# Gated attention: the output of block 2 by seven products, the ranking cut into pieces between its additions

## The chip, the cores and the metric

The kernel runs on one core of a Trainium2 chip. The metric is the device time of one execution in microseconds (us), the median of several runs. The engines are TensorE (PE, with its weight loads as PEld), VectorE (DVE), ScalarE (ACT), GpSimd (POOL) and the queue that issues most transfers (SP). Each engine works through its own list of instructions in order, and waits where an instruction needs something of another engine.

## The reference, cut to what matters

Two layers, each of attention and a feed-forward part with a layer norm behind each, on an input of 2 × 1024 rows of 512. The change lies in the second layer, between its gated attention and its feed-forward part:

```python
go = o @ Wog.T + x @ Wig.T
on = o * lax.rsqrt(jnp.mean(o * o, axis=-1, keepdims=True) + EPS) * g_norm_w
o = on * (go * jax.nn.sigmoid(go))
return o @ Wo.T                       # the gated attention's output, added to x, then normed
...
scores = jnp.einsum('bsd,d->bs', hidden_states, router_weight) + router_bias[0]
top_scores, indices = jax.lax.top_k(scores, K)          # K = 512 of 1024 rows per batch
selected = jnp.take_along_axis(hidden_states, indices[:, :, None], axis=1)
h = jax.nn.gelu(jnp.einsum('bkd,df->bkf', selected, w1) + b1)
processed = jnp.einsum('bkf,fd->bkd', h, w2) + b2
out = flat.at[flat_idx].add(weighted.reshape(b * K, d))
```

Only the 512 rows of each batch with the highest scores pass the feed-forward part.

## The kernel before, in words

The 2048 rows are four blocks of 512, two for each batch; a block is four tiles of 128 rows. In the second layer a loop `for blk in range(NB)` takes one block after the other, with these steps, all in fp32:

- `attend(blk)` makes the attention's rows o: PE products into four PSUM banks (`op`, L1389 and L1369 in `inside`). ACT copies each bank to `oT` (L1406) and squares it (L1397) into a tile of the pool `jk` with the tag "junk"; POOL adds the squares up (L1398, L1399) into `sum2`. `rms(blk, sum2)` (products `mp` L1415, DVE L1417, POOL L1418) makes `inv[blk]` of it.
- `gate(blk)` is a generator that makes u, the gated rows, by Strassen's products in Winograd's form: seven products of half-size blocks in place of eight (PE `go`, L921), two of which grow in one PSUM bank. It needs two sums beside o: `o_sum(blk)` (DVE L1421) and `other_sums(blk)` (DVE L1425 and L1426). DVE adds the products up in `uT` (L1471, L1472, L1488), ACT applies silu (L1491, L1442, L1490), and DVE multiplies by o and the weight of the norm (L1445 in `end`, two pairs of two). `uT` is one tile that all blocks share.
- The output u · Wo is added to x, scaled by `inv`. Blocks 0 and 1 take `sums_of_u()` (DVE L1506 to L1508) and then `finish_by_seven` while the next block is in the gate: again seven products (PE L1521), of which `grow` is a bank in which four grow one after the other. DVE reads the bank after each (L1530, two additions of 256 columns), and the next product on it waits for that read. Blocks 2 and 3 take `finish(blk)`: 16 matmuls of 512 columns into four banks `ao` (PE L1561), with no sums; DVE adds each bank to x (L1565) and takes statistics (L230, L231).
- `scored_rows(blk)` norms the rows (L217, POOL's power L218, L223) and makes the scores (L1581). `route(b, room)` is a generator that ranks a batch's 1024 rows once its two blocks are scored: transposes of the scores (PE `rp` L1603, ACT L1604), then for each of eight tiles of rows comparisons with all scores on DVE (L1614, L1617, L1620), whose junk output `cmp` takes a tile of the tag "junk" too. After every second tile the ranks become indices (L1626, L1627), and POOL issues two indirect DMAs (L1629) that write the picked rows to `picked[b]`.
- `fetch(0)` reads the picked rows back in 16 transfers on SP, `turn_picked` transposes them on DVE (L1663), `sums_of_x` makes their sums for the feed-forward products (L1670 to L1673), `sums_of_w1` those of the weights (L2068). `hidden(0, ...)` is the first feed-forward product (PE `hp`, L1696).

The pool `jk` has two buffers for the tag "junk": a new tile of that tag waits until the last but one has been read. They are handed out in the order in which the code is recorded.

The order of the instructions on each engine is made by a scheduler from the recorded code, with its own estimate of when things are ready. Two means hold it: PE's products are chained by hand (`last_3[0]`), and `with tc.issue_after(ins)` keeps all that is recorded in it behind `ins` on the engine of `ins`.

Batch 0 is ranked while block 3 is attended to. In the kernel before, its generator is advanced in block 2's gate, three steps behind an addition there and six behind the next, so that all eight tiles' comparisons are recorded ahead of `attend(3)`:

```python
            if blk == 2 and n:
                if n < 3:
                    added = done
                with tc.issue_after(added if n == 2 else done):
                    for _ in range((0, 0, 3, 6)[n]):
                        next(ranking)
```

Of the kernel before, what the change touches and what calls it, by code (L numbers as in the profile page):

```python
# [10 lines left out]
F32 = mybir.dt.float32  # L11
# [10 lines left out]
P = 128  # L22
B, T, C = 2, 1024, 512
NB = 4
# [48 lines left out]
def body(ctx: ExitStack, tc: tile.TileContext, a: dict, out: bass.AP):  # L73
    nc = tc.nc
# [88 lines left out]
    t, src = new_xT(0)  # L163
# [1125 lines left out]
    def new_front(blk, gates, *bank):  # L1289
        return front(blk, gates, wk.tile([P, 4, P], F32, tag="ex", name="ex"), *bank)  # L1290
# [129 lines left out]
    def o_sum(blk):  # L1420
        return nc.vector.tensor_sub(gR["T2"], oT[blk][:, :, 256:], gR["T1"]).ins  # L1421
# [130 lines left out]
    def finish(blk):  # L1552


        ao = [acc_bank("ao3") for _ in range(4)]
        steps = [(i, n) for i in range(4) for n in range(4)]
        if blk == NB - 1:
            steps = [(0, 0), (0, 1), (1, 0), (1, 1), (0, 2), (0, 3), (1, 2), (1, 3)] + steps[8:]
        for i, n in steps:
            k = (0, 2, 1, 3)[n]  # L1560
            last_3[0] = nc.tensor.matmul(ao[i], uT[blk][:, k, i * P : (i + 1) * P], W1o[:, k], start=n == 0, stop=n == 3).ins  # L1561
        mv = sp.tile([P, 4, 2], F32, tag="mv", name="mv")
        for i in range(4):
            x = x_t[blk][:, i]
            nc.vector.scalar_tensor_tensor(x, ao[i], inv[blk][:, i : i + 1], x, ALU.mult, ALU.add)  # L1565
            row_stats(mv[:, i], x)
        return scored_rows(blk, mv)
# [98 lines left out]
    def sums_of_x(x, room):  # L1666
        T = room.rearrange("p (i k) (h t) -> p i k h t", k=2, h=2)
        T1, T2, T3, T4 = (T[:, i // 2, :, i % 2] for i in range(4))
        B11, B12, B21, B22 = x[:, :2, :256], x[:, :2, 256:], x[:, 2:, :256], x[:, 2:, 256:]
        nc.vector.tensor_sub(T1, B12, B11)  # L1670
        nc.vector.tensor_sub(T2, B22, T1)
        nc.vector.tensor_sub(T4, T2, B21)
        nc.vector.tensor_sub(T3, B22, B12)  # L1673
        return (B11, B21, B22), (T1, T2, T3, T4)

    turns, last_hp = [0], [None]

# [255 lines left out]
    now.power()  # L1933
    with tc.issue_after(scored):
        next(ending)
    for blk in range(NB):
        if blk == 1 or blk == 2:
            with tc.issue_after(ended) if blk == 1 else contextlib.nullcontext():
                *sums, summed = sums_of_u()
            if blk == 1:  # L1940
                with tc.issue_after(summed):
                    turned = summed = turn_late(3)
                with tc.issue_after(summed):
                    W1o_sums, summed = sums_of_W1o()
                w1 = w34.tile([P, KC, DFF], F32, tag="w1", name="w1")
                nc.sync.dma_start(out=w1, in_=a["w1"].rearrange("(k p) f -> p k f", p=P))
                w1v = w1.rearrange("p k (j e f) -> p k j e f", e=2, f=P)
                wA11, wA12, wA21, wA22 = w1v[:, :2, :, 0], w1v[:, 2:, :, 0], w1v[:, :2, :, 1], w1v[:, 2:, :, 1]
                wS3 = wA21
        with tc.issue_after(last_3[0]) if blk == 1 else contextlib.nullcontext():  # L1950
            sum2 = attend(blk)
        if blk == 2:
            with tc.issue_after(last_op[0]):
                new_front(3, gates, acc_bank)
        if blk == 1:
            last_3[0] = last_op[0]
        if blk:
            with tc.issue_after(summed) if blk == 1 else contextlib.nullcontext():
                o_sum(blk)
            gating = gate(blk)  # L1960
            if blk < 3:
                finishing = finish_by_seven(blk - 1, sums, W1o_sums, turned if blk == 1 else None)
                for n in range(2):
                    next(finishing)
                    if blk == 1 and n == 0:
                        last_turned[0] = last_3[0]
                        lT = logits(1, jk.tile([P, 512], F32, tag="junk", name="lT"))
                        last_3[0] = last_turned[0]
                    next(gating)
                    if blk == 1 and n == 0:  # L1970
                        with tc.issue_after(last_3[0]):
                            lp = turned_logits(lT)
                        last_3[0] = last_turned[0]
                        gates = Gates([wk.tile([P, 8, 32], F32, tag=t, name=t) for t in ("q3", "k3", "l3")])
                        gates.whole(lp)
                added = last_add[0]
                next(finishing)
                if blk == 1:
                    with tc.issue_after(last_3[0]):
                        last_3[0] = gates.decayed(kd_room, jk.tile([P, 8, 32], F32, tag="junk", name="e3"))  # L1980
                    turn_of["mm"] += 1
                    with tc.issue_after(last_3[0]):
                        last_3[0] = new_front(2, gates)
                next(finishing)
                with tc.issue_after(last_3[0]):
                    part = scores(blk + 1, gates)
                    next(part)
                last_3[0] = last_tp[0]
                next(finishing)
            else:  # L1990
                scored = finish(blk - 1)
                for _ in range(2):
                    next(gating)
        next(gating)
        if blk:
            rms(blk, sum2)
        if blk == 0:
            part = scores(1, gates)
            next(part)
        elif blk < 3:  # L2000
            scored_next = next(part)
        if blk == 2:
            with tc.issue_after(scored_next):
                scored = scored_rows(1)
            ranking = route(0, xT_tile("row"))
        if blk == 0:
            summed = o_sum(0)
            nc.sync.dma_start(out=rw, in_=a["rw"].to_broadcast([P, C]))
            nc.sync.dma_start(out=b2, in_=a["b2"].to_broadcast([P, C]))
        if blk == 1:  # L2010
            with tc.issue_after(scored_next):
                rooted = root_of_rows(0)
        if blk == 0:
            with tc.issue_after(summed):
                added = next(ending)
            put_rows(3, "x2r")
            get_squares(3, "x2r", squares_of_x2(3))
        with tc.issue_after(summed if blk == 1 else added) if blk < 3 else contextlib.nullcontext():
            other_sums(blk)
        if blk == 0:  # L2020
            next(gating)
            scored_next = next(part)
        if blk == 3:
            xsS = fetch(0)
            with tc.issue_after(scored):
                rooted = root_of_rows(0, 0.25e-5)
        for n, done in enumerate(gating):
            if n == blk == 0:
                rms(0, sum2)
            if n == 2 and blk == 0:  # L2030
                with tc.issue_after(done):
                    x_sum(1)
                    turn_late(2)
                with tc.issue_after(last_3[0]):
                    inside(1, 0)
                last_3[0] = last_op[0]
            if n == 1 and 0 < blk < 3:
                with tc.issue_after(done):
                    x_sum(blk + 1)
            if n == 3 and blk == 1:  # L2040
                with tc.issue_after(done):
                    scored_rows(0, None, rooted)
            if n == 1 and blk == 3:
                with tc.issue_after(done):
                    unpicked(0, rooted)
                p7_added = done
            if n == 3 and blk == 0:
                ended = done
            if blk == 2 and n:
                if n < 3:  # L2050
                    added = done
                with tc.issue_after(added if n == 2 else done):
                    for _ in range((0, 0, 3, 6)[n]):
                        next(ranking)
    wS1, wS2, wS4 = (spare[i][:, :, :512].rearrange("p (k h) (j f) -> p k h j f", h=2, f=P) for i in range(3))

    def pair_of(w, g):
# [12 lines left out]

    xs = xT_tile("xsT")
    with tc.issue_after(p7_added):
        sums_of_w1((0,))
        turn_picked(xs, xsS)
    xs = sums_of_x(xs, W1oT)
    finish(3)
    with tc.issue_after(p7_added):
        sums_of_w1((1,))
    s3.close()
    wk = ctx.enter_context(tc.tile_pool(name="s4", bufs=2))  # L2080
# [21 lines left out]
        return turn_picked(room, later[0])  # L2102

    def next_sums():
        later.append(sums_of_x(room, x_room(0, "xsums")))

    def first_ranks():
        rank_some(4)
# [66 lines left out]
```

## Time and profile before

| | us |
|---|---|
| median of 3 runs | 873.0 |
| lowest and highest run | 872.01, 873.72 |
| the profiled execution | 872.3 |
| its span, first to last instruction | 870.5 |
| PE busy in it | 861.3 (99%) |
| DVE busy in it | 681.4 (78%) |
| PE's granted clock | 0.999 of full speed |

The profile is of one execution. "Busy" counts the time in which an engine works on an instruction. The chain of waits goes back from the last instruction: at each step to what released it, or to the instruction before it on its engine. The timeline has the instructions of an engine in order of time. All times inside the execution count from the start of the span; block 3's attention starts at 611.17, and the feed-forward part at 668.58.

### The profile page before, as it was taken

Reading aid. Unit: us, or ns where it says so; the run is one execution under the profiler, and the core shown is the slowest. Engines: PE = TensorE matmul, PEld = TensorE weight load, DVE = VectorE, ACT = ScalarE, POOL = GpSimd, SP = SyncE. Lnnn points to the kernel's source line nnn. Section 1 sums busy time; section 2 is a strip of 40 time slices with the busy share of each in tenths; the row PEclk is TensorE's granted clock in tenths of the full one; section 3 lists DMA queues with packets and bytes.
Section 4 is the critical chain, followed back from the end, with each engine's and each line's share of the span. In section 5 each row is a group of like instructions: output and inputs, shape, how many; then the busy total and the mean of one; then the engine's idle time right before and its main releaser. Section 6 shows DMA issues by size and latency. Waiting matters only on the chain.

```text
span 870.5 us, 11281 instructions
## 1 busy us (share of the span) xinstructions
PE 861.3 (99%) x4067; PEld 682.9 (78%) x4067; DVE 681.4 (78%) x1340; ACT 373.7 (43%) x636; POOL 265.0 (30%) x249
## 2 busy tenths in 40 slices
PE   9999999999999999999999999999999999999996
PEld 6667886678578888888887787888686888888885
DVE  3668984988877788887787988677988988998525
ACT  2345333453468797787886624132210222210000
POOL 2120020830474367457556312030520210000112
PEclk9999999999999999999999999999999999999999
DMA  9632212210241302504301654000154140320001
GB/s 336 225 104 66 82 50 78 73 49 12 68 152 49 49 1 55 91 1 120 75 0 37 133 99 193 1 1 1 38 117 161 50 74 28 118 97 1 25 24 49
DMA packets 103848, 64.87 MB, mean 75 GB/s; under 512 B 80078, under 2 KB 80634, under 8 KB 103281
## 3 DMA queue, kind: packets, MB, share of 16 engines
q1 hardware_dynamic: 101153, 58.89, 24.0%
q0 software_dynamic: 1920, 4.22, 1.3%
q10 hardware_dynamic: 720, 1.05, 0.4%
q8 instruction: 32, 0.52, 0.3%
q14 instruction: 23, 0.19, 0.1%
HBM read 48.37 MB, written 17.88 MB: 76 GB/s over the span
## 4 chain that ended last, share of the span: by engine, by line
PE 88%; issue 4%; POOL 3%; DVE 3%; DMA 1%; POOLq 0%; ACT 0%; DVEq 0%
PE hp L1696 11%; PE yp L1790 11%; PE go L921 10%; PE yp L953 9%; PE gatep L953 9%; PE upp L953 9%; PE grow L396 4%; PE xk L448 4%; PE P L396 3%; PE ao L1561 3%; PE grow L572 2%; POOL x L223 2%; PE kp L646 2%; PE P L572 2%; PE grow L1521 2%
## 5 line engine op out<-in xcount | busy, mean ns | idle before, releaser
L1018 DVE TENSOR_TENSOR yp<-yp,ratio 128x512 f32<-128x512 f32 x160 | 103.2, 693 | 18.2 <-PE yp L953 16.2
L978 ACT ACTIVATE gatep<-gatep,scale 128x512 f32<-128x512 f32 x132 | 84.0, 659 | 36.3 <-PE gatep L953 33.3
L218 POOL TENSOR_TENSOR rs<-rs,table 128x4 f32<-128x4 f32 (+1 forms) x19 | 16.6, 875 | 251.2 <-DVE rs L217 250.9
L953 PE MATMUL yp<-wdn,hhi 128*128 128x512 f32 x176 | 70.3, 399 | 0.2 <-DVE yp L1018 0.2
L953 PE MATMUL gatep<-x1Th,wgu 128*128 128x512 f32 x176 | 70.3, 400 | 0.0
L953 PE MATMUL yp<-wdn,hlo 128*128 128x512 f32 x176 | 69.9, 397 | 0.2 <-POOL hlo L987 0.2
L953 PE MATMUL gatep<-x1Tl,wgu 128*128 128x512 f32 x176 | 69.1, 393 | 0.0
L953 PE MATMUL upp<-x1Tl,wgu 128*128 128x512 f32 x176 | 68.9, 391 | 0.0
L953 PE MATMUL upp<-x1Th,wgu 128*128 128x512 f32 x176 | 68.9, 391 | 0.0
L978 ACT ACTIVATE upp<-upp,scale 128x512 f32<-128x512 f32 x100 | 64.8, 663 | 6.6 <-PE upp L953 3.1
L987 POOL TENSOR_TENSOR hlo<-whole,hhi 128x512 fp32r<-128x512 f32 x43 | 55.5, 1291 | 3.5
L986 POOL CAST hhi<-whole 128x512 fp32r<-128x512 f32 x43 | 26.3, 611 | 86.4 <-DVE whole L984 85.7
L984 DVE SCALAR_TENSOR_TENSOR whole<-upp,scale,silu 128x512 f32<-128x512 f32 x43 | 32.3, 750 | 19.8 <-PE upp L953 12.2
L921 PE MATMUL go<-spare,spare 128*128 128x256 f32 x192 | 44.1, 382 | 0.0
L448 PE MATMUL xk<-pair,x 128*128 128x512 f32 x96 | 42.7, 592 | 0.0
L230 DVE BATCH_NORM_STATS2 st<-x 128x6 f32<-128x512 f32 x64 | 42.3, 676 | 0.3
L953 PEld LDWEIGHTS yp<-wdn,hhi 128*128 128x128 f32 x176 | 33.1, 188 | 10.3 <-DVE yp L1018 1.3
L953 PEld LDWEIGHTS gatep<-x1Th,wgu 128*128 128x128 f32 x176 | 33.1, 188 | 9.1 <-ACT gatep L978 1.1
L921 PEld LDWEIGHTS go<-spare,spare 128*128 128x128 f32 x192 | 36.1, 190 | 5.1
L953 PEld LDWEIGHTS yp<-wdn,hlo 128*128 128x128 f32 x176 | 33.1, 188 | 7.8 <-POOL hlo L987 0.6
L953 PEld LDWEIGHTS gatep<-x1Tl,wgu 128*128 128x128 f32 x176 | 33.1, 188 | 7.5 <-issue 0.2
L953 PEld LDWEIGHTS upp<-x1Th,wgu 128*128 128x128 f32 x176 | 33.1, 188 | 7.3 <-DVE rw L984 0.2
(461 smaller groups left out, 2036.2 us busy)
## 6 DMA issues: line engine op xcount, KB each, us to landing
pk<-in_gu SPq DMA_DIRECT2D x16, 352.0 KB, 3.6
x<-in_x SPq DMA_DIRECT2D x4, 1024.0 KB, 14.1
w<-in_w SPq DMA_DIRECT2D x1, 4096.0 KB, 12.6
w<-in_w SPq DMA_DIRECT2D x4, 1024.0 KB, 5.3
out<-x SPq DMA_DIRECT2D x4, 1024.0 KB, 4.2
x0T<-in_xT SPq DMA_DIRECT2D x3, 1024.0 KB, 7.3
x1r<-x SPq DMA_DIRECT2D x3, 1024.0 KB, 4.3
x1S<-x1r SPq DMA_DIRECT2D x12, 256.0 KB, 4.5
```

The source lines that it names most:

```text
L230: nc.vector.bn_stats(st, x)
L396: ins = nc.tensor.matmul(ps[:, 256 * r : 256 * r + 256], a[:, k, r * P : (r + 1) * P], b[:, k], start=first and r == 0 and k == 0, stop=k ...
L448: ins = nc.tensor.matmul(acc_of[b][c], x_t[blk][:, i, c * P : (c + 1) * P], pairs_of["k", blk][i // 2][:, i % 2], start=blk % 2 == 0 and i ...
L572: ins = nc.tensor.matmul(ps[:, 256 * r : 256 * r + 256], a[:, k, r * P : (r + 1) * P], b[:, k], start=first and r == 0 and k == 0, stop=k ...
L921: ins = nc.tensor.matmul(ps[:, 256 * m : 256 * m + 256], w[:, k, m], b[:, k, 256 * half : 256 * half + 256], start=first and m == 0 and k ...
L953: nc.tensor.matmul(ps, w, x, start=start and n == 0, stop=stop and n == 1, skip_group_check=True)
L978: nc.scalar.activation(ps, ps, AF.Copy, scale=s)
L984: nc.vector.scalar_tensor_tensor(self.whole, ps, s, self.silu, ALU.mult, ALU.mult)
L987: nc.gpsimd.tensor_sub(lo, self.whole, hi.bitcast(F32))
L1018: nc.vector.tensor_tensor(self.y[:, i] if g == NI - 1 else ps, ps, ratio[:, g], ALU.mult)
L1696: ins = nc.tensor.matmul(ps[:, 256 * j : 256 * j + 256], pair_of(w, g)[:, k, j], x[:, k], start=k == 0, stop=k == 1).ins
L1790: nc.tensor.matmul(ps[:, 256 * r : 256 * r + 256], x(r, j), w(j), start=j == 0, stop=j == NJ - 1)
```

## The change

- Block 2's output goes through `sums_of_u()` and `finish_by_seven` as well, between the steps of block 3's gate. `finish` is left for block 3 alone.
- Of the ranking of batch 0, three steps (transposes, comparisons 0 and 1) stay in block 2's gate. The other six are recorded in block 3: two behind the sums of u, one behind the first pair of products' additions, two behind the next, one behind the last addition. `attend(3)` is now recorded between comparison 1 and comparison 2.
- `o_sum(3)` is recorded behind the additions of block 2 instead of ahead of them; statistics and scores of block 2 follow by `scored_rows(2)`.
- Behind the addition of block 3's gate called `p7_added`, the first sums of w1, the transposes of the picked rows and the sums of x are chained, each behind the last of the one before, and `finish(3)` and the second sums of w1 behind those.

The generators are not changed, but for `sums_of_x`, which also returns its last instruction. From the lines of `finish` on, a line of the changed kernel has a number lower by one; from the main loop on they differ more (the sums of w1 are L2076).

```diff
@@ in finish
-        if blk == NB - 1:
-            steps = [(0, 0), (0, 1), (1, 0), (1, 1), (0, 2), (0, 3), (1, 2), (1, 3)] + steps[8:]
+        steps = [(0, 0), (0, 1), (1, 0), (1, 1), (0, 2), (0, 3), (1, 2), (1, 3)] + steps[8:]
@@ ahead of the loop over the blocks
+    def rank_behind(ins, n):
+        with tc.issue_after(ins):
+            for _ in range(n):
+                next(ranking)
+
     for blk in range(NB):
-        if blk == 1 or blk == 2:
+        if blk:
             with tc.issue_after(ended) if blk == 1 else contextlib.nullcontext():
                 *sums, summed = sums_of_u()
...
         if blk:
             with tc.issue_after(summed) if blk == 1 else contextlib.nullcontext():
-                o_sum(blk)
+                if blk < 3:
+                    o_sum(blk)
             gating = gate(blk)
+            finishing = finish_by_seven(blk - 1, sums, W1o_sums, turned if blk == 1 else None)
+            if blk == 3:
+                rank_behind(summed, 2)
+            for n in range(2):
+                next(finishing)
+                if blk == 3:
+                    rank_behind(last_add[0], (1, 2)[n])
...
+                next(gating)
...
+            added = last_add[0]
+            next(finishing)
...
+            next(finishing)
             if blk < 3:
...
                 with tc.issue_after(last_3[0]):
                     part = scores(blk + 1, gates)
                     next(part)
                 last_3[0] = last_tp[0]
-                next(finishing)
-            else:
-                scored = finish(blk - 1)
-                for _ in range(2):
-                    next(gating)
+            next(finishing)
+            if blk == 3:
+                added = last_add[0]
+                o_sum(3)
+                rank_behind(added, 1)
+                scored = scored_rows(2)
...
-        with tc.issue_after(summed if blk == 1 else added) if blk < 3 else contextlib.nullcontext():
+        with tc.issue_after(summed if blk == 1 else added):
             other_sums(blk)
...
-            if blk == 2 and n:
-                if n < 3:
-                    added = done
-                with tc.issue_after(added if n == 2 else done):
-                    for _ in range((0, 0, 3, 6)[n]):
-                        next(ranking)
+            if blk == 2 and n == 1:
+                added = done
+            if blk == 2 and n == 2:
+                rank_behind(added, 3)
...
     xs = xT_tile("xsT")
     with tc.issue_after(p7_added):
-        sums_of_w1((0,))
-        turn_picked(xs, xsS)
-    xs = sums_of_x(xs, W1oT)
-    finish(3)
-    with tc.issue_after(p7_added):
+        ins = sums_of_w1((0,))
+    with tc.issue_after(ins):
+        ins = turn_picked(xs, xsS)
+    with tc.issue_after(ins):
+        *xs, ins = sums_of_x(xs, W1oT)
+    with tc.issue_after(ins):
+        finish(3)
         sums_of_w1((1,))
```

## The prediction

> **What bounds the kernel now.** I read the page first (which engine is full), then the chain of waits around the changed block, then busy time by stretch there, then that block's timeline on VectorE (DVE), ScalarE (ACT) and GpSimd (POOL). TensorE is PE. Times are us on the axis of the profiled execution.
>
> ```profile
> PE 861.3 (99%) x4067; PEld 682.9 (78%) x4067; DVE 681.4 (78%) x1340; ACT 373.7 (43%) x636; POOL 265.0 (30%) x249
> ```
>
> PE sets the time; a gain has to be taken from PE, and a loss shows where PE begins to wait. The chain, in order of time (start, length):
>
> ```profile
> 611.17 1.10 PE op L1389 x32
> 612.27 3.77 PE op L1369 x32
> 616.04 13.74 PE ao L1561 x32
> 629.78 6.91 PE go L921 x32
> 636.68 0.79 PE mp L1415 x8
> 637.47 17.38 PE go L921 x80
> 654.84 13.73 PE ao L1561 x32
> 668.58 10.36 PE hp L1696 x48
> ```
>
> The `ao` at 616.04 is finish(2), what changes; the one at 654.84 is finish(3). Every piece is PE, end to end: nothing waits. The price of a product by sevens is in the same chain, where block 1 is finished in that way:
>
> ```profile
> 571.44 1.73 PE grow L1521 x8
> ```
>
> Busy time by stretch (length, PE, PEld, DVE, ACT, POOL):
>
> ```profile
> 611.00:637.50 26.50, 26.50 (x138) 17.83 (x138) 25.06 (x73) 6.10 (x11) 15.70 (x18) 1.00 0.11 41
> 637.50:654.80 17.30, 17.30 (x81) 15.26 (x81) 14.36 (x35) 2.27 (x3) 2.02 (x2) 1.00 0.74 177
> ```
>
> While `ao` runs, DVE is full too (25.06 of 26.50): it ranks, and PE waits for none of it. That independence is what the change gives up. Rows that give prices, from the timeline (start, length, what, and in brackets the idle time before it and who ended it), first of POOL, then of DVE:
>
> ```profile
> 615.22 1.23 POOL L1629 DMA_INDIRECT picked<-x,index  x1 [14.97 <-DVE index L1627]
> 616.75 0.98 POOL L1629 DMA_INDIRECT picked<-x,index  x1 [0.30 <-issue]
> ...
> 625.49 2.74 POOL L1398 TENSOR_TENSOR sq<-sq 128x256 f32<-128x256 f32 x2
> ...
> 631.22 0.73 POOL L1398 TENSOR_TENSOR sq<-sq 128x256 f32<-128x256 f32 x1
> 632.02 0.45 POOL L1399 TENSOR_TENSOR sum<-sq 128x128 f32<-128x128 f32 x1
> ```
> ```profile
> 637.09 1.91 DVE L223 TENSOR_SCALAR x<-x,mv,rs 128x512 f32<-128x512 f32 x4 [1.16 <-POOL rs L218]
> ...
> 648.04 0.69 DVE L1472 TENSOR_TENSOR uT<-uT,go 128x512 f32<-128x512 f32 x1 [2.76 <-PE go L921]
> ...
> 653.48 1.41 DVE L1445 SCALAR_TENSOR_TENSOR uT<-spare,gw,uT 128x512 f32<-128x512 f32 x2
> ```
>
> One half-addition on POOL (L1398) takes 0.73 or 1.37. The first L1445 pair of block 3 ends at 654.81 and the last `ao` starts at 654.84: DVE is only just in time there already.
>
> **What PE saves.** 16 matmuls of 512 columns, 13.74, become 7 products of 1.73 (four matmuls of 256 columns each), 12.1: −1.65. Nothing else on PE changes. That is 0.19% of 873.0, inside the 0.2% that a measurement of this kernel can tell from no change: even kept whole it is no visible gain.
>
> **What DVE gains in work.** Three sums of u and one more subtraction, 4 × 0.60 = 2.4; 14 additions of 256 columns at 0.40 (L1530 pairs: 0.80) for 4 of 512 at 0.66: +2.95. Together +5.35. Moved behind the L1445 pairs, by the new pinning of the picked rows' turn and the sums of w1: 3 sums (1.8) and 2 transposes (1.3) that stood before the last pair.
>
> **What new waits arise.** The built order of the changed kernel shows them. Both the rank comparisons and the squares of attend use the tag "junk" with two buffers. Before, all comparisons were recorded ahead of attend(3), so the squares waited for them (ACT at 623.33, 624.95) and nothing on PE cared. Now attend(3) lies after comparison 1 and before comparison 2. In order:
> - POOL issues the first two indirect DMAs until 617.73 as before; then all four squares' additions follow (before: after six DMAs).
> - ACT runs copy, square, copy, square, copy from 614.92; square 2 needs the buffer of square 0, so POOL's sum 0. DVE idles then, so POOL's short rows apply: 0.73 + 0.08 + 0.46 = 1.27 less overlaps, 1.24 a square. Sum 0 is done at 619.0, sum 1 at 620.25. Square 2 and, behind it, copy 3 (0.5 + 0.6) end at 620.15.
> - DVE ends the three sums of u at 616.9 and has o_sum(3) (L1421) next, which needs copy 3: it stands still from 616.9 to 620.2, 3.3 lost on the fullest queue. L1421 takes 1.2 to 1.74.
> - Comparison 2 needs sum 2, comparison 3 needs sum 3. POOL's sum 2 runs beside L1421, a two-input addition. Bounds: 1.24 (the short rows) to 2.57 (block 1's slow ones under the same L1421: 1.17 + 0.08 + 1.32); I take 2.05, as its first row is surely beside L1421 and the second is not. Sum 3 runs beside a comparison; 1.24 to 2.24, I take 1.3, since no row shows a comparison slowing POOL. Comparison 2 then starts at 620.25 + 2.05 = 622.3, and comparison 3, for which sum 3 is ready at 623.6, behind it at 624.1, with 0.2 for the hand-over (1.61 each: 0.40 + 0.93 + 0.27, and 0.53 + 0.80 + 0.27).
> - Behind them on DVE stand the two additions that read `grow` (0.95 with the small rank steps). PE's third product accumulates on that bank and waits for both: it starts at T = 624.1 + 1.61 + 0.95 = 626.7. Low end: sums of 1.24, comparison 2 at 621.55, T = 625.7. High end: sum 3 at 620.25 + 2.57 + 2.24 = 625.05, T = 627.6, with 0.3 for slower DMA issue 627.9. PE has then done A11·B11, A12·B21 and the gate's first product (616.04 + 1.73 + 1.73 + 3.45) at 622.95: it waits 3.75.
>
> The Trainium skill ("SBUF — State Buffer", Who interferes with whom) says that a VectorE instruction with two SBUF inputs blocks a GpSimd one that reads SBUF, and that the accumulating form of tensor_scalar does not. It would give T some 626.9; the rows above (1.37 beside L1421 and L1425, 0.73 apart) agree for the first half, and for the second no row here shows it.
>
> **From T to the last `ao`.** PE: five products and the gate's second, 5 × 1.73 + 3.45 = 12.1, ends A12·B22 at T + 12.1 = 638.8 (each reads a bank that DVE frees about 1 earlier). DVE is paced by PE up to there; then its own queue holds, by rows: last two additions 0.80, comparison 7 1.61, statistics of block 2 with the rank's end 2.9, L1425 1.14, L217 to L223 with POOL's power 1.33, L223 1.83, scores 2.45, statistics of block 0 2.85, L1471 and L1472 1.2, L217 to L223 1.33, L223 1.83, first L1445 0.74: 20.0. PE's gate products and mp need only 18.06, and wait on the way: the last gate product for L1472 (about 1.7) and `ao` for L1445 (0.3). So `ao` starts at T + 12.1 + 0.1 + 20.0 = T + 32.2 = 658.9 against 654.84: +4.1 (bounds +3.1 and +5.3).
>
> The skill's "Perfetto Trace Analysis" (Identifying the Most-Contended Engine) says to find the fullest engine and optimize it first; by it alone the sum would be −1.65. The row with DVE at 25.06 of 26.50 speaks against that here.
>
> **What follows.** Ranking ends at 642.7 instead of 628; its last DMA is issued at 645.1 (635.0), the 16 fetches (8.31, begun 1.7 later, 2.3 to land) are in by 657.4. The transposes, now behind the L1445 pairs, start at 663.3 and the sums of x are complete at 668.9; `hp` starts at 672.6: covered by 3.7, lost one for one if that cover is gone. SP's w2 loads and the write of block 0 wait behind those fetches; their users come over 90 later. Block 3's scores now carry four sums of w1 before them: done 9.7 after `hp` starts (before: 8.2), needed at 10.36 by the ranking's transposes, the second of which also needs a bank freed at 10.4. That may cost 0 to 0.5; I take 0. From there on the order is as before. Sum: 872.3 (span 870.5 and 1.8 around it) + 4.1 = 876.4; the median shown is 0.7 above this execution, so 877.1.
>
> **Rivals.** (1) The saving is kept: 873.0 − 1.65 = 871.35, no visible change. Mechanism: POOL's square sums free the two junk buffers early. It decides from where comparison 3 starts by 620.4, so that T is 622.95. For: POOL's additions are short and its spans rough. Against: POOL is in the indirect DMAs until 617.73, four squares follow it, and DVE's 20.0 would also have to shrink by 1.95. (2) The wait on `grow` is gone but DVE's queue is not: T = 622.95 gives +0.3, 873.3, no change. For: the second half stands on short, well-known rows. Against: the same as in (1). (3) POOL's slow rows everywhere, and the bank at `rp`: +5.3 + 0.5, 878.8; it belongs to the upper end.
>
> **Numbers.** Forecast with its bounds, and (3): 0.86. Rival (2): 0.07. Rival (1): 0.04, and 0.03 for the same with 0.1 or more on top, which a measurement would call faster. Faster 0.03, same 0.11 (1 and 2), slower 0.86. The range: 873.0 + 3.1 less 1.0 (the runs' spread below the median) = 875.1, to 878.8 + 0.7 (their spread above) = 879.5; it leaves out (1) and (2).
>
> **What would show it.** In the profile after: L1421 of block 3 waits some 3.3 for ACT; PE has a gap of 3 to 5 in front of the third product of block 2, released by DVE L1530; DVE almost without gaps from 639 to 659; a second PE gap of about 2 before the last gate product or `ao`; `hp` starting 4 later, with no gap. Wrong if that first gap is under 1, or if `hp` waits for the picked rows.

## The result: slower by 1.1%, twice what was forecast

| | before | after |
|---|---|---|
| median, us | 872.66 (4 runs) | 881.85 (4 runs) |
| lowest and highest run | 872.01, 873.72 | 880.96, 883.84 |
| profiled execution | 872.30 | 881.12 |
| its span | 870.5 | 879.3 |
| PE's granted clock in it | 0.999 | 0.996 |

The ratio of the medians is 1.011 (95% interval 1.010 to 1.0124). The forecast was 877.1 (875.1 to 879.5): the direction is right, the loss of 9.2 is more than twice the 4.1 to 4.4 forecast (877.1 less 873.0 or 872.66).

The page's line of busy time:

```profile
PE 862.8 (98%) x4091; PEld 687.7 (78%) x4091; DVE 683.7 (78%) x1354; ACT 373.3 (42%) x636; POOL 265.7 (30%) x249
```

PE's busy time rose by 1.5, although it has less to do; why, the granted clock shows below. The waits of PE from 560 on (line that waited, who ended it, us in total, times, longest):

```profile
PE grow L1521 <- DVE x L1530: 4.0, 1, 4.0
PE go L921 <- DVE uT L1472: 3.2, 1, 3.2
PE hp L1695 <- DVE xsums L1670: 0.3, 1, 0.3
```

From 560 on, the profile before has no such line. PE's timeline at these places (start, length, what, in brackets the idle time before it and who ended it): the third product of block 2, the end of the seven, the last product of block 3's gate, the last `ao`, the first `hp`.

```profile
627.25 3.65 PE L1521 MATMUL grow<-spare,uS 128*128 128x256 f32 x8 [4.01 <-DVE x L1530]
641.09 0.95 PE L1415 MATMUL mp<-table,sum 128*128 128x1 f32 x8
...
659.13 3.72 PE L921 MATMUL go<-spare,Wog 128*128 128x256 f32 x16 [3.16 <-DVE uT L1472]
662.90 14.00 PE L1560 MATMUL ao<-W1o,uT 128*128 128x512 f32 x32
676.74 3.62 PE L1695 MATMUL hp<-xsT,w 128*128 128x256 f32 x16
```

The third product (`grow`, S2·T2) took 3.65; the same form took 1.89 elsewhere (the next one starts 1.73 behind it, before its modelled end). The busy time by stretch says why (length, PE, PEld, DVE, ACT, POOL, then the granted clock, DMA share, GB/s):

```profile
625.00:630.00 5.00, 2.75 (x7) 2.22 (x8) 5.00 (x18) 0.00 (x0) 1.97 (x2) 0.72 0.08 28
630.00:635.00 5.00, 5.00 (x23) 4.39 (x22) 3.46 (x11) 0.00 (x0) 0.00 (x0) 0.94 0.08 29
```

The granted clock was 0.72 and 0.94 in these two stretches, and 1.00 in all stretches of 5 us around them: 5 × 0.28 + 5 × 0.06 = 1.7 us of PE's time. In the trace's clock records it is one fall to half, 3.413 us long, that begins at 627.22, at the end of the gap of 4.01.

What VectorE did at the two gaps:

```profile
620.66 1.23 DVE L1421 TENSOR_TENSOR spare<-spare,spare 128x1024 f32<-128x1024 f32 x1 [3.49 <-ACT spare L1406]
623.04 0.48 DVE L1613 TENSOR_SCALAR_CACHE_REDUCE cmp<-row,score 128x256 bf16<-128x256 f32 x1 [1.15 <-POOL sum L1399]
...
647.67 0.16 DVE L217 TENSOR_SCALAR rs<-mv 128x4 f32<-128x4 f32 x1
...
650.88 1.92 DVE L223 TENSOR_SCALAR x<-x,mv,rs 128x512 f32<-128x512 f32 x4 [1.92 <-POOL rs L218]
```

And GpSimd:

```profile
620.70 1.77 POOL L1398 TENSOR_TENSOR sq<-sq 128x256 f32<-128x256 f32 x1
...
622.96 0.72 POOL L1398 TENSOR_TENSOR sq<-sq 128x256 f32<-128x256 f32 x1
...
645.38 0.97 POOL L1628 DMA_INDIRECT picked<-x,index  x1 [0.77 <-DVE mv L231]
646.66 1.94 POOL L1628 DMA_INDIRECT picked<-x,index  x1 [0.30 <-issue]
648.61 1.25 POOL L1418 TENSOR_TENSOR ms<-ms,table 128x4 f32<-128x4 f32 x1
649.85 1.00 POOL L218 TENSOR_TENSOR rs<-rs,table 128x4 f32<-128x4 f32 x1
```

The first two rows of DVE are the waits forecast: L1421 stood 3.49 for ACT's copy, comparison 2 stood 1.15 for POOL's sum. The last two were not forecast: from L217 to L223 DVE needs POOL's power L218, and POOL had ahead of it two indirect DMAs of the ranking (the second 1.94 instead of 0.97) and the power of `rms` (L1418, 1.25). From L217 to L223 it took 3.21. In the kernel before it took 1.33 (635.76 to 637.09), with nothing ahead of the power:

```profile
635.76 0.17 DVE L217 TENSOR_SCALAR rs<-mv 128x4 f32<-128x4 f32 x1
636.01 1.04 POOL L218 TENSOR_TENSOR rs<-rs,table 128x4 f32<-128x4 f32 x1 [1.01 <-DVE rs L217]
```

### The profile page after: what moved, and what is told of

The parts are those of the page before. It is cut to its first block, busy times and chain, and to the rows that moved or that the text cites. A ratio compares the mean times of both kernels' runs of the same rounds, so it can differ in the third digit from the quotient of the medians.

```text
span 879.3 us, 11345 instructions
## 1 busy us (share of the span) xinstructions
PE 862.8 (98%) x4091; PEld 687.7 (78%) x4091; DVE 683.7 (78%) x1354; ACT 373.3 (42%) x636; POOL 265.7 (30%) x249
## 4 chain that ended last, share of the span: by engine, by line
PE 80%; DVE 8%; issue 6%; POOL 3%; SPq 1%; DMA 1%; ACT 0%; POOLq 0%; DVEq 0%
PE yp L1789 11%; PE yp L953 9%; PE gatep L953 9%; PE upp L953 9%; PE xk L448 6%; PE grow L396 6%; PE hp L1695 5%; PE go L921 5%; PE P L396 4%; PE grow L1521 2%; PE grow L572 2%; PE P L572 2%; PE kp L646 2%; PE P L1521 2%; SPq L1654 1%
## 5 line engine op out<-in xcount | busy, mean ns | idle before, releaser
L218 POOL TENSOR_TENSOR rs<-rs,table 128x4 f32<-128x4 f32 (+1 forms) x19 | 17.0, 892 | 252.5 <-DVE rs L217 252.1
```

## The experiments

Each kernel was timed beside the kernel before on the same chip, with several runs of each (the medians of before were 872.74, 872.02 and 872.52 in the three groups). "From op" counts from the start of block 3's `op` in the same trace, which takes out a start that differs between executions by up to 2.3; the last `ao` starts 43.58 from op before, and 51.52 after; the end comes at 259.42 before, and 267.96 after.

### Own buffers for the comparisons

```diff
-            cmp = jk.tile([P, T], BF16, tag="junk", name="cmp")
+            cmp = jk.tile([P, T], BF16, tag="cmp", name="cmp")
```

> The comparisons' junk output gets buffers of its own, so attend's squares no longer wait for comparisons nor comparisons for POOL's sums of squares. Theory (the shared junk buffers make DVE late at grow): the gap of PE in front of the third product of block 2 falls from 4.0 to under 0.5, PE's granted clock stays at 1.0 there, and ao of block 3 starts about 2.4 later than in the kernel before instead of 8; the time is about 875.5. Rival (DVE's added work alone makes the loss, the buffers only decide where the wait shows): the gap moves to the gate's last products and the time stays at 881 to 882.

Measured: 877.96 (ratio 1.0054, 1.0037 to 1.0071). The gap at `grow` is gone, as the theory has it: the third product follows the gate's first at once, at 11.74 from op (15.87 after). Almost four of the nine us were the shared buffers. But the time is 2.5 over the expectation, and `ao` starts 3.63 later from op than before, not 2.4. The second gap stayed at 3.2, and now the clock fell there:

```profile
653.62 5.41 PE L921 MATMUL go<-spare,Wog 128*128 128x256 f32 x16 [3.16 <-DVE uT L1472]
```
```profile
655.00:660.00 5.00, 5.00 (x15) 3.63 (x14) 3.91 (x8) 0.93 (x2) 0.00 (x0) 0.68 0.58 174
```

The gate's last product took 5.41 instead of 3.72, at a granted clock of 0.68 in the stretch from 655. In the changed kernel a gap of the same 3.16 at the same place cost no clock. So the gap and the fall of the clock are two different prices, and here the fall came at the next gap.

### The gap filled with repeated work

```diff
-            p1 = product(one, gA[11], x, 0, True)
+            for _ in range(2 if blk == 3 else 1):
+                p1 = product(one, gA[11], x, 0, True)
             yield
```

> The gate's first product of block 3 is computed twice, 3.45 of repeated work that PE does just where it waits 4.0 for DVE; nothing else changes. Theory (the wait itself costs 3.75, and the clock that falls to one half behind it another 1.7): no window with a granted clock of 0.72, the third product takes 1.9 instead of 3.65, the time is about 1.7 lower, 880.1. Rival (that product was long for another reason, a weight load or a bank): it stays at 3.65 and the time at 881.9.

Measured: 881.41. The third product took 1.99, so its length was the clock's doing and not a bank's or a weight load's. But next to nothing was gained (0.44): the half clock came 31 us later, behind the second gap of 3.17, where the gate's last product took 5.35. The expectation had not reckoned with that.

```profile
627.76 1.99 PE L1522 MATMUL grow<-spare,uS 128*128 128x256 f32 x8 [0.56 <-DVE x L1531]
...
657.99 5.35 PE L921 MATMUL go<-spare,Wog 128*128 128x256 f32 x16 [3.17 <-DVE uT L1473]
```

### The last indirect DMAs behind the power

```diff
+                if b == 0 and i == 7:
+                    yield
                 for n in (i - 1, i):
                     ins = nc.gpsimd.indirect_dma_start(
...
                 scored = scored_rows(2)
+                with tc.issue_after(last_pow[0]):
+                    next(ranking)
```

> Only POOL's order differs: the last two indirect DMAs of batch 0 are issued behind the power (L218) of block 2's statistics instead of ahead of it. Theory (the power stood queued behind them): L217 to L223 takes 1.3 instead of 3.2, ao of block 3 starts 1.5 to 1.9 earlier, the time is 880.0 to 880.4. Rival (DVE's later queue absorbs it, or the picked rows come too late for hp): the time stays at 881.9, and in the second case hp waits for the transposed picked rows.

Measured: 881.49, a median over runs at unlike clocks: at a mean of 0.996 they took 880.21 and 880.32, at 0.993 and 0.991 882.67 and 883.04. In the profiled executions, both with one fall of the clock, it is 880.21 against 881.12. POOL in this kernel:

```profile
646.11 2.02 POOL L1418 TENSOR_TENSOR ms<-ms,table 128x4 f32<-128x4 f32 x1 [2.02 <-DVE mv L231]
648.12 1.18 POOL L218 TENSOR_TENSOR rs<-rs,table 128x4 f32<-128x4 f32 x1
649.48 1.04 POOL L1630 DMA_INDIRECT picked<-x,index  x1 [0.18 <-issue]
```

L217 to L223 took 2.18 instead of 3.21, not the 1.3 expected: L1418 still stands ahead of the power, and took 2.02 there. So of the 1.88 that the step grew over its 1.33 in the kernel before, 1.03 goes with the indirect DMAs and 0.85 stays with L1418 ahead of the power. The second gap shrank to 2.20, and `ao` starts 1.2 earlier from op. `hp` did not wait for the picked rows.

### Without the pins

```diff
-        ins = sums_of_w1((0,))
-    with tc.issue_after(ins):
-        ins = turn_picked(xs, xsS)
-    with tc.issue_after(ins):
-        *xs, ins = sums_of_x(xs, W1oT)
-    with tc.issue_after(ins):
-        finish(3)
-        sums_of_w1((1,))
+        sums_of_w1((0,))
+        turn_picked(xs, xsS)
+    *xs, ins = sums_of_x(xs, W1oT)
+    finish(3)
+    with tc.issue_after(p7_added):
+        sums_of_w1((1,))
```

> The pins of the picked rows' turn, of the sums of w1 and of x and of finish(3) at the end of the change are taken out; the recording order there is that of the kernel before. Theory: the pins are free or a gain; without them DVE's transposes and sums of x stand behind other work of block 3, and hp waits for them by 2 to 5: 884 to 887. Rival (the pins cost time, since they hold three sums and two transposes behind the last additions of uT): 1 to 2 faster, 880 to 881.

Measured: 885.56 (ratio 1.0139, 1.0121 to 1.0157), as the theory has it. The pins earn 3.7 between the medians. Without them there is one more wait of PE:

```profile
PE hp L1695 <- DVE xsT L1662: 2.8, 1, 2.8
```

The clock was at half for 10.2 us in all in the profiled execution, three times the changed kernel's, so part of the 3.7 is the clock's. The two runs with a mean clock of 0.997 took 883.58 and 884.41, still 2.5 to 3.5 above the changed kernel's two at 0.996.

### Both gaps filled

```diff
-        p2 = lambda: nc.vector.tensor_add(c11, c11, product(acc_bank("go"), gA[12], oT[blk], 0, True)).ins
+        def p2():
+            ps = acc_bank("go")
+            for _ in range(2 if blk == 3 else 1):
+                y = product(ps, gA[12], oT[blk], 0, True)
+            return nc.vector.tensor_add(c11, c11, y).ins
```

(on top of the first gap's filling)

> The changed kernel, with work repeated in both gaps: the gate's first product and its third product (gA12 by oT) of block 3 are computed twice, 3.45 each, so PE never idles there. The waits for VectorE are as they were. Theory (the clock's fall costs 1.7 once in the changed kernel, in the one gap or in the other): no half clock anywhere, ao of block 3 starts 1.5 to 1.9 earlier than in the changed kernel, and the time is 880.0 to 880.5. Rival (the clock has no part in the loss): 881.9.

Measured: 882.21, which is near the rival's number, for another reason. The clock did not fall, and the gate's last product started at 46.23 from op (47.75 after), 1.5 earlier, the size that the theory gives for `ao`. But a new wait ate it, and `ao` itself started at 52.06 (51.52 after):

```profile
PE ao L1565 <- DVE uT L1445: 2.2, 1, 2.2
```

The repeated product pushed the gate's product behind it by 3.45. So that product's addition came behind L223 on VectorE, at 660.81, and ACT's silu and L1445 behind that. The run does not tell the theories apart.

### One gap filled, the other under 3 us

The two small edits together, the first gap filled and the indirect DMAs behind the power.

> Both small edits at once: the gate's first product of block 3 computed twice (fills the first gap), and the last two indirect DMAs issued behind the power of block 2's statistics (which cut the second gap from 3.2 to 2.2). Each alone gained 0.4 or less. Theory (the clock falls once for a gap of 3.2 or more, wherever it is, and not for 2.2): no window at half clock, and the two together gain more than their sum, 1.7 + 1.0 to 1.5: 878.6 to 879.2. Rival (no part of the loss is the clock's): their sum, about 881.

Measured: 879.37 (ratio 1.0083, 1.0068 to 1.0099). Alone the two edits gained 0.44 and 0.36, together 2.48. In the profiled execution the clock does not fall at all, with these waits:

```profile
PE go L921 <- DVE uT L1473: 2.2, 1, 2.2
PE grow L1522 <- DVE x L1531: 0.6, 1, 0.6
PE hp L1698 <- DVE xsums L1673: 0.3, 1, 0.3
```

From op to the end it is 265.42, 2.54 under the changed kernel. In the profiled executions of the two edits alone, each with one fall of the clock, it was 0.03 and 0.67 under it. So together they gain 1.84 more than their sum, about one fall (1.7), and the rival (their sum, 881) is ruled out.

### The ranking in one piece

```diff
-            if blk == 3:
-                rank_behind(summed, 2)
...
-                if blk == 3:
-                    rank_behind(last_add[0], (1, 2)[n])
...
-                rank_behind(added, 1)
...
+            if blk == 2 and n == 3:
+                rank_behind(done, 6)
```

> The changed kernel with one part of the change undone: all six comparisons of the ranking stand again in one piece ahead of the sums of u, as in the kernel before, and none between the additions. Theory (VectorE's work has to be somewhere): the third product waits for six comparisons and three sums, T near 628 to 629 and a gap of 5 to 6 with the clock's fall, but VectorE is short of work later, so the second gap of 3.2 is gone: 879 to 881. Rival (the pieces are what costs the time): back to 873 to 875.

Measured: 880.85 (ratio 1.0101, 1.0086 to 1.0117), so the rival is ruled out: without the pieces it is only 1.0 less, and most of the loss remains. But the mechanism was not the one expected. PE waits at the second product, not the third, and for ACT:

```profile
623.99 3.71 PE L1521 MATMUL P<-W1o,uT 128*128 128x256 f32 x8 [6.21 <-ACT sq L1397]
```

And ACT waits for a comparison, for the junk buffer:

```profile
623.34 0.60 ACT L1397 ACTIVATE sq<-op 128x512 f32<-128x512 f32 x1 [6.36 <-DVE cmp L1619]
```

The product's bank is one that a square has yet to read. The third product starts at 19.87 from op, 4.0 later than in the changed kernel; the second gap is 0.40, as expected. The half clock lasted 6.8 us here, twice as long as in the changed kernel, so the two kernels also differ by a price of the clock.

### The seventh comparison earlier

```diff
-                    rank_behind(last_add[0], (1, 2)[n])
+                    rank_behind(last_add[0], (1, 3)[n])
...
                 o_sum(3)
-                rank_behind(added, 1)
```

First with the buffers shared as in the changed kernel:

> The changed kernel with only the seventh comparison one piece earlier, the junk buffers shared as in the changed kernel. Theory: the first gap of 4.0 and the clock's fall behind it stay, the second gap of 3.2 falls to 0 or near it: 3 less, 878.3 to 879.3. Rival (the two gaps are one loss, seen twice): the time stays at 881 or more.

Measured: 878.20 (ratio 1.0074, 1.0059 to 1.0089). The first gap stays at 4.01, with its half clock; the second falls from 3.16 to 0.40. The edit does two things there: L217 to L223 took 2.19, 1.02 less, since the last two indirect DMAs are issued earlier, and the comparison's own 1.60 no longer stands between the last addition and L1445. Then with own buffers:

> The comparisons have buffers of their own, and besides them the seventh comparison stands one piece earlier, ahead of the last three pairs of additions, where VectorE waits for TensorE anyway; so the last two indirect DMAs also leave POOL before the power of block 2's statistics. Theory (VectorE's own queue makes the second gap: 1.6 of comparison and 1.9 of a power that stands behind indirect DMAs): the gap of 3.2 before the gate's last product falls to under 0.7, the clock stays at 1.0, ao of block 3 starts within 0.7 of the kernel before; 873 to 873.8, no visible change from before. Rival (the gap is made elsewhere, by the squares or the statistics of block 0): a gap of 2 or more stays, 876 to 878.

Measured: 872.98 (ratio 1.0013, 1.0004 to 1.0022): one tag and one comparison's place take 8.2 of the 9.2 away. The clock does not fall. What is left in the profile is a wait of 1.1 where the comparison now stands ahead of an addition to `grow`, 0.4 before the gate's last product, and 0.5 at `xsums`.

### Towards a version that gains

Three kernels, all with own buffers for the comparisons. The first two have the seventh comparison one piece earlier, as above, and put the second statistics of block 0 (2.85 on DVE) between the additions; the second of them also puts block 0's last normalization behind L1445. The third is like the second, but with the seventh comparison behind the third pair of additions and the statistics behind the fourth. Its edit, without the tag of the buffers:

```diff
             next(finishing)
+            if blk == 3:
+                rank_behind(last_add[0], 1)
...
             next(finishing)
+            if blk == 3:
+                with tc.issue_after(last_add[0]):
+                    rooted = root_of_rows(0, 0.25e-5)
...
                 o_sum(3)
-                rank_behind(added, 1)
...
             xsS = fetch(0)
-            with tc.issue_after(scored):
-                rooted = root_of_rows(0, 0.25e-5)
...
             if n == 1 and blk == 3:
-                with tc.issue_after(done):
-                    unpicked(0, rooted)
                 p7_added = done
+            if n == 3 and blk == 3:
+                with tc.issue_after(done):
+                    unpicked(0, rooted)
```

> The kernel with own buffers and the seventh comparison earlier, and also the second statistics of block 0 (2.85 of VectorE) between the additions instead of behind block 2's scores. Theory (everything VectorE does between the last addition and the first L1445 pair counts one for one): no gap in front of the gate's last product, ao of block 3 starts 1.3 or more earlier than in the kernel before (its saving of 1.65 less some 0.3), and the time is 871.4 to 872.4, at or just below the kernel before. Rival (the picked rows now bound it, so a gain there is given back at hp): ao starts earlier, but hp or the sums of x wait, and the time is 873 or more.

> As the one with the statistics earlier, and the last normalization of block 0's rows (L223 four times, 1.92) and the write of those rows stand behind the L1445 pairs instead of ahead of them. Theory: ao of block 3 starts up to 0.5 earlier still, 871.0 to 872.0. Rival (the write of block 0 on SP, or the normalization among the sums of w1 and the transposes, delays hp): 872.5 or more, with a wait before hp.

> The kernel with own buffers, early statistics and late rows of block 0, with the seventh comparison behind the third pair of additions instead of ahead of it, and the statistics of block 0 behind the fourth: no addition to grow stands behind a comparison any more. Theory: the wait of 0.5 before the last product is gone, ao of block 3 starts 0.4 to 0.6 earlier, 872.3 to 872.7, level with the kernel before or just above it, since about 0.8 is lost behind hp in all of these kernels. Rival (the wait moves to the gate's last product): no gain, 873.1.

Measured: 872.92 (1.0008, 0.9999 to 1.0017), 873.06 (1.0008, 0.9998 to 1.0017) and 872.05 (0.9998, 0.9989 to 1.0007). The first two missed: `ao` starts only 0.49 earlier from op than before, since the wait at `grow` was still 0.52, and the normalization's place made no difference. From `hp` to the end they took 202.92 and 202.99 (202.11 before), so more than the gain was given back there, as the first one's rival has it, with 0.47 of it a wait for `xsums`. The third has these waits left:

```profile
PE hp L1695 <- DVE xsums L1670: 0.5, 1, 0.5
PE go L921 <- DVE uT L1472: 0.3, 1, 0.3
```

Its `ao` starts 42.70 from op, 0.88 earlier than before; from `hp` to the end it is 202.76 against 202.11. So 0.65 goes there, 0.47 of it the wait for `xsums`, whose picked rows of batch 1 come later. It is level with the kernel before; none of these kernels beat it.

## Why the prediction was right in kind and wrong in size

By its steps, in the profiled execution. `op` starts 0.28 later than before (611.38 against 611.10 in the timeline), ahead of all that the change touches. The chain's 654.84 for `ao` is 654.68 in the timeline, so the forecast of 658.9 is 658.74 there, and T = 626.7 is 626.54. (T itself was added up from timeline rows, so 0.16 of its miss below is only the step between the two axes.)

- **PE's saving, 1.65**: the products took 1.73 each, from start to start, as priced, where the clock was full. In the last kernel, which has no wait over 0.2 between the seven products, `ao` starts 0.88 earlier and one wait of 0.33 is on view; the other 0.44 of the saving went into waits too short for the view. What they are stays open.
- **The junk buffers, T**: right. L1421 stood 3.49 (forecast 3.3), comparison 2 waited for POOL's sum, and the third product started 0.43 after the forecast, allowing for the 0.28. The gap was 4.01 (3.75). The kernel with own buffers shows that it was they. POOL's third sum took 2.26 from start to start, where 2.05 was taken: its row beside L1421 took 1.77. The next row, beside comparison 2, took its usual 0.72. That agrees with the half of the Trainium skill's rule ("SBUF — State Buffer", Who interferes with whom) that no row of before showed: the accumulating comparison did not slow POOL.
- **From T to `ao`, 32.2: the term that failed**, by 3.45, in two places.
  - PE's 12.1 was 13.84 (627.25 to 641.09). The sum carried a gap of 3.75 and priced it at its own length; the half clock behind it cost another 1.74. No row of before showed it, for PE had no such gap there. The filled gap shows the slow product to be the clock's, and the pair of small edits shows that about 1.7 of it lasts to the end.
  - DVE's 20.0 was 21.7. L217 to L223 was priced at 1.33 from the place where POOL was free. In the changed order the last ranks become indices just ahead, and their DMAs, and `rms`'s power, stand in POOL's queue: 3.21. The prediction listed these DMAs and when they are issued, but only to time the picked rows; it did not ask who stands behind them on POOL. The rest of DVE's queue came out 0.17 shorter.
- **The second gap**: forecast at 1.7 before the last gate product, and 0.3 at `ao`; measured 3.16 and none over 0.2. The 1.88 of POOL more than covers the difference: with the last indirect DMAs behind the power, 1.03 less there took 0.96 off this gap.
- **The pins**: right. `hp` had no wait for the picked rows; without the pins it waits 2.77.
- **0 to 0.5 behind `hp`, taken as 0**: measured 0.49 (202.60 against 202.11), of which 0.32 is a wait for `xsums`, which the prediction did not list, and 0.11 is at `rp`, where it looked (from there to the next product 0.99 against 0.88).
- **The rest**: from the profiled execution's 8.82 to the medians' 9.19. Of the four runs two had a mean clock of 0.996, the others 0.993 and 0.991, and these took 1.5 to 2.9 longer. At 0.002 for each stretch at half clock, as in the trace, that would be one to three such stretches more, an estimate: these runs left no trace, so it is not shown.

Sum: 0.28 + 4.06 (the forecast) + 0.43 + 1.74 + 1.71 + 0.11 (`ao` to `hp`) + 0.49 = 8.82.

Rival (2), the wait on `grow` gone and VectorE's queue as it is, is the kernel with own buffers alone. It was priced at 0.3 and measured at 5.2: from the third product to `ao` took 35.47 there, by the same two prices that the forecast's 32.2 left out. Rival (1), the saving kept, no kernel showed; with VectorE's later queue thinned as well, the last one is level with before. Rival (3), slow rows on POOL, named the right engine, but not the rows.

## What to carry to other kernels

A wait that a change brings to a full PE is priced by its length and by the clock behind it (1.7 here); with two gaps, closing one may bring next to nothing, as the clock then falls at the other. When instructions are moved, look up each queue that they land in for who comes next there: here two DMA issues put a power 1.0 us back, and the power the gate's last product. And a scratch tag shared by two loops is an order between them: a tag of its own was worth 3.9 us here, beside a saving of 1.65.

## What the runs showed of the hardware

- PE's clock falls to half for 3.413 us, or twice that, and the times between its changes are whole multiples of that (in the changed kernel 182 and 72 of them), but for the last stretch, which ends with the trace. A gap of 4.01 brought the fall in each profiled execution that had one (the changed kernel and three others); one of 3.16 or 3.17 did in three of four, and 2.2 and 2.77 did not. Laid over the gaps, these windows of 3.413 suggest that it goes by how the gap falls into them: 1.97 of idle time in one window brought no fall (the changed kernel's second gap) and 2.26 did (the kernel with own buffers). The clock stayed at half for two windows where the fall came with 1.11 or 3.33 of the gap still to go (without the pins, ranking in one piece), and for one where at most 0.57 was left. The Trainium skill ("TensorE: Matmul & The Clock Gate", Part 1) gives the same free-running window of 3413 ns, but asks for a whole idle window of about 3.4 us; gaps of 3.16 were enough here, and the measurement decides.
- An indirect DMA's issue on POOL took 1.94 instead of 0.97 while VectorE ran L1425 and L1426, each of two SBUF inputs, beside it, in the changed kernel and again in the one with own buffers.
